# Causal attention: the mask on the transposed scores moves from a TensorE product to a GpSimd select on the exponentials

## The chip, the cores and the metric

The kernel runs on one core of a Trainium2 chip. The metric is the device time of one execution in microseconds (us). The kernel before took 5578.49 us, the median of three runs (5568.84 to 5580.77 us).

## The reference

The program is a chain of twelve layers over an input of 8 sequences x 256 tokens x 128 features in f32. Each layer normalises its input and adds its result to it: mixtures of experts, a recurrent layer, a local attention network of depth 6, and three attentions with 16 heads of 8 features. Only two of the attentions are causal, and only these are touched.

The first one is an ordinary causal softmax attention:

```
scores = einsum('bhqk,bhsk->bhqs', q, k) / sqrt(dk)
causal_mask = triu(ones((s, s), bool), k=1)
scores = where(causal_mask, -1e9, scores)
weights = softmax(scores, -1)
ctx = einsum('bhqs,bhsk->bhqk', weights, v)
```

The last one has rotated queries and keys in the numerator and plain ones in the denominator; the denominator sums over all keys, the mask applies to the quotient only:

```
num = exp(einsum('bhqd,bhkd->bhqk', q_rot, k_rot) * scale)
den = sum(exp(einsum('bhqd,bhkd->bhqk', q, k) * scale), -1, keepdims=True)
attn = where(tril(ones((C, C), bool)), num / den, 0.0)
```

## The kernel before

The 2048 tokens are cut into four groups of two sequences (512 tokens); activations stand with features on the partitions and tokens along the row. The stages run one after the other, and pieces of the neighbouring stage (normalisations, for instance) are drawn from a queue by `pump` (line 438) and put between the products of the present one.

An attention stage (`attention`, line 953) walks over 16 *quads*, that is, four heads of one group, in a software pipeline: step t projects quad t, does the score products of quads before it, and finishes quads still further back. Inside a stage the order on every compute engine is the order of the program: the class `_Ordered` (line 285) chains each instruction of VectorE (DVE), ScalarE (ACT), GpSimd (POOL) and TensorE (PE) to the one issued before it on that engine. So an instruction that waits holds back all later ones of its engine.

In a step there are four *pairs*. A pair handles two heads of one sequence of 256 tokens:

- First attention (`softmax_quads`, line 812; `pair`, line 850). For quad q1 the scores are computed with queries on the partitions (tile `ms`), and DVE takes the largest of each row (`a_mneg`, line 831). In the next step, quad q2, whose maxima are then known and have been folded into its queries (`a_qa`, made in `turn`, line 843), has its scores computed once more with keys on the partitions (tile `ss`), and ACT takes the exponential of them into `a_e` (`soft`, line 756).
- Last attention (`rotated_quads`, line 892; `pair`, line 912). No maxima are needed: `ms` holds the rotated scores, whose exponential goes to `a_e`, and `ss` the plain ones, whose exponential goes to `a_n` and is summed by DVE into the denominator `a_den`.

A tile of `ms`, `ss` or of the projection `pp` takes two banks of PSUM, and three such tiles exist (`mm2=3` in lines 1688 and 1715). Two more banks serve everything else: one accumulator for `av`, and one called `bank`, which holds in turn the transposed tiles, the output projection and the parts of the queue.

With keys on the partitions, the 256 keys of a sequence are two halves of 128. A pair's `ss` (in the last attention its `ms`) holds for each head 384 columns: the first half of the keys against all 256 queries, then the second half against the last 128 queries. The first and the third 128 columns are diagonal blocks, in which the keys behind a query have to go. The function `scores` (line 727) does this on TensorE: ahead of the score products it multiplies a bf16 identity with a bf16 table that holds 0 or -2^100 (`cq` for queries on the partitions, `ck` for keys on the partitions), once per head with 256 columns, as the first term of the sum in PSUM. The score products (f32, 32-row products in four row groups) are added to it, and the exponential turns the rest into zero. The tables are made from f32 constants by `low_masks` (line 700) at the start of each stage, on DVE.

The exponentials are used in `weigh` (line 761), which multiplies them with the values into `av`. It is called twice per quad: for the first sequence right after pair 2 of the same step (line 885 and line 945), and for the second in the next step, after that step's projection (line 875 and line 933). In the first attention the transposes of the maxima (`turn`) stand between. `weighed` copies `av`, `divide` transposes it, divides by the sum of weights and writes `a_ctx`.

GpSimd has in the first attention only the memsets of `value_rows` (line 691) and `max_rows` (line 709) at the start of the stage, and in the last one the memsets and two products for each rotation (lines 1023 and 1026).

Of the kernel before, what the change touches and what calls it, by code (L numbers as in the profile page):

```python
# [24 lines left out]
ALU = mybir.AluOpType  # L25
# [3 lines left out]
P = 128  # L29
# [11 lines left out]
NEG = -float(2.0**100)  # L41
# [11 lines left out]
def _constants():  # L53

    f = np.float32
    p = np.arange(P)
    c = {}
    c["ident"] = np.eye(P, dtype=f)
    c["mean"] = np.full((P, P), 1.0 / P, f)
    c["ones"] = np.ones((P, P), f)  # L60
    c["iota"] = np.tile(np.arange(E, dtype=f), (P, 1))
    c["krow"] = (p % 32 == DH).astype(f)[:, None]
    c["eps"] = np.tile(
        np.array([1e-5, 2e-5, 2.0**-64, 0.5 * SH * math.log(2.0)], f), (P, 1)
    )
    blk = (p[:, None] // 64 == p[None, :] // 64).astype(f)
    c["blkm"] = blk / f(64)

    z = np.zeros((P, 32), f)
    z[:64, :16] = 1.0  # L70
    z[64:, 16:] = 1.0
    c["hsum"] = z
    z = np.zeros((P, 4), f)
    for n, r in enumerate((32, 96, 48, 112)):
        z[r, n] = 1.0
    c["hpick"] = z

    r = np.zeros((P, P), f)
    for m in range(P):
        if m % 2 == 0:  # L80
            r[m + 1, m] = -1.0
        else:
            r[m - 1, m] = 1.0
    c["rot2"] = r

    sel = np.zeros((P, 4, P), f)
    for g in range(4):
        for j in range(4):
            for d in range(DH):
                sel[DH * (4 * g + j) + d, g, 32 * j + d] = 1.0  # L90
    c["sel"] = sel.reshape(P, -1)


    lev = [np.eye(P, dtype=f)]
    for i in range(7):
        n = 2**i
        q = p // n
        lev.append(((q[:, None] % 2 == 0) & (q[None, :] == q[:, None] + 1)).astype(f))
    c["lev"] = np.concatenate(lev, 1)

    c["cq"] = np.where(p[None, :] > p[:, None], f(NEG), f(0))
    c["ck"] = np.where(p[:, None] > p[None, :], f(NEG), f(0))
    one9 = np.zeros((P, 32), f)
    one9[:, DH] = 1.0
    c["one9"] = one9


    i, key = np.arange(32), np.arange(64)
    ok = (key[None, :] >= i[:, None]) & (key[None, :] <= i[:, None] + WIN)
    m = np.zeros((2, 2, 32, 2, 64), f)  # L110
    m[:, 0] = np.where(ok, f(0), f(LNEG))[:, None, :]
    m[:, 1, :, 0, :WIN] = LNEG
    c["lmask"] = m.reshape(P, -1)
    m = np.zeros((2, 2, 32, 4, 32), f)
    m[:, 0] = np.eye(32, dtype=f)[:, None, :]
    m[:, 1, :, 0] = np.eye(32, dtype=f)
    c["lrow"] = m.reshape(P, -1)

    half = np.arange(0, 64, 2, dtype=f)
    inv_freq = f(1.0) / f(10000.0) ** (half / f(64))  # L120
    t = np.arange(S, dtype=f)
    fr = t[:, None] * inv_freq[None, :]
    fr = np.concatenate([fr, fr], -1).T
    base = (half + f(0.4 * 64)) / f(1.4 * 64)
    sc = base[None, :] ** ((t - f(S // 2)) / f(WIN // 2))[:, None]
    sc = np.concatenate([sc, sc], -1).T
    two = lambda a: np.concatenate([_partners(a.T).T] * 2, 0).astype(f)

    sgn = np.where(p[:64, None] < 32, f(-1), f(1))
    c["qcos"] = two(np.cos(fr) * sc * f(8.0))  # L130
    c["qsin"] = two(np.sin(fr) * sc * f(8.0) * sgn)
    c["kcos"] = two(np.cos(fr) * (f(1.0) / sc))
    c["ksin"] = two(np.sin(fr) * (f(1.0) / sc) * sgn)

    i = np.arange(DH // 2, dtype=f)
    th = np.power(f(10000.0), f(-2.0) * (i - f(1.0)) / f(DH))
    ang = t[:, None] * th[None, :]
    per = lambda a: np.tile(np.repeat(a.T, 2, axis=0), (NH, 1)).astype(f)
    c["rcos"] = per(np.cos(ang))
    c["rsin"] = per(np.sin(ang))  # L140

    groups = {
        "c1": ("ident", "mean", "ones", "iota", "krow", "eps"),
        "cs0": ("cq", "ck"),
        "cs1": ("lev", "blkm"),
        "cs2": ("hsum", "hpick", "lmask", "lrow", "qcos", "qsin", "kcos", "ksin"),
        "cs3": ("rot2", "sel", "ck", "one9", "rcos", "rsin"),
    }
    return {n: {k: c[k].astype(f) for k in ks} for n, ks in groups.items()}

# [9 lines left out]
def _partners(w):  # L160

    w = np.asarray(w)
    return w.reshape(w.shape[:-1] + (2, 32)).swapaxes(-1, -2).reshape(w.shape)
# [16 lines left out]
def _layout(inp):  # L180
# [74 lines left out]
    }  # L255
    a, at = {}, {}
    packs = {"pv": pv, "w0": w0, "wt": wt, "w1": w1, "w2": w2, "w3": w3, **_constants()}
    for name, parts in packs.items():
        a[name], at[name] = _pack(parts)
# [49 lines left out]
class _Net:  # L309
# [417 lines left out]
    def scores(self, jobs):  # L727

        parts = {
            None: ((0, 0, 0, S), (1, S, 0, S)),
            "cq": ((0, 0, 0, P), (1, S, 0, S)),
            "ck": ((0, 0, 0, S), (1, S, P, P)),
        }
        for st, a, c, b, heads, mask in jobs:
            if mask is None:
                continue
            for h in range(2):
                blocks = st[:, h, :].rearrange("p (x k) -> p x k", x=4)  # L740
                self.nc.tensor.matmul(
                    blocks[:, 0 :: 3 if mask == "cq" else 2, :], lhsT=self.low["ident"],
                    rhs=self.low[mask].unsqueeze(1).to_broadcast([P, 2, P]),
                    start=True, stop=False, skip_group_check=True)
        for part in range(2):
            for st, a, c, b, heads, mask in jobs:
                half, at, c0, n = parts[mask][part]
                o = b * S
                for h, j in enumerate(heads):
                    r = slice(32 * j, 32 * j + 32)  # L750
                    self.nc.tensor.matmul(
                        st[:, h, at : at + n], lhsT=a[r, o + P * half : o + P * (half + 1)],
                        rhs=c[r, o + c0 : o + c0 + n], start=mask is None, stop=True,
                        skip_group_check=mask is not None)

    def soft(self, st, n):
        e = self.work("a_e", (P, 2, T), bufs=6)
        self.act(e[:, :, :n], st[:, :, :n], AF.Exp, scale=1.0 / math.sqrt(DH))
        return e

    def weigh(self, q, b, causal):
# [532 lines left out]
    def two(self, name):  # L1294
        return self.psp2.tile([P, 2, T], F32, tag="mm2", name=name)
# [383 lines left out]
    def run(self, stages):  # L1679
# [7 lines left out]
        def att0(st):  # L1687
            self.scope(st, "a0", mm=0, acc=1, mm2=3)
            self.value_rows()
            self.max_rows()  # L1690
            self.low_masks(("ident", "cq", "ck"))
            self.attn0()

        def rwkv(st):
# [19 lines left out]
        def att3(st):  # L1714
            self.scope(st, "a3", mm=0, acc=1, mm2=3)
            self.value_rows(ones=False)
            self.low_masks(("ident", "ck"))
            self.attn3()

        makers = (moe0, att0, moe0, None, rwkv, None, local, att2, local, moe3, att3, moe3)  # L1720
        for g in range(NG):
            self.queue.append(self.enter(0, g))
# [56 lines left out]
```

## Time and profile before

| What | Value |
|---|---|
| median of the runs | 5578.49 us |
| the profiled execution | 5561.13 us, span 5559.4 us |
| granted TensorE clock, mean | 0.962 |
| busy share of the span | PE 90%, weight loads 54%, DVE 63%, ACT 44%, POOL 42% |
| first attention | about 275 to 505 us: PE busy 206.5, DVE 110.8, ACT 82.7, POOL 6.2 us |
| last attention | about 5086 to 5374 us: PE busy 241.0, DVE 153.0, ACT 118.1, POOL 25.6 us |
| mask products with `ck` | 128 in each of the two, 0.27 us each as recorded (they overlap) |
| exponentials `a_e` of 768 elements | 64 in each of the two, 0.81 us each |
| maxima `a_mneg` of a pair | 0.42 and 0.68 us as recorded, 1.02 us together |

A line of the groups view names the source line, the engine, the operation, and the tiles as written<-read, with shapes, count, busy time and mean; the line number is mostly that of the helper that records every operation (L300), so the tiles tell the operations apart. A line of the timeline gives start and duration in us; several equal instructions in a row are merged (x2), and the bracket at the end tells how long the engine had been idle before and what released it. The durations of matrix products overlap, so their starts tell more than their lengths. An f32 product is recorded as two.

### The profile page before, as it was taken

To read this page: it belongs to the slowest core of one execution; us is meant where nothing else is said; L and a number is where in the kernel's file an instruction comes from. 1 tells how busy PE (TensorE), PEld (TensorE's weight loads), DVE (VectorE), ACT (ScalarE), POOL (GpSimd) and SP (SyncE) were. 2 spreads that over 40 slices of the span, in tenths; PEclk is the share of its full clock that TensorE was granted. 3 is DMA by queue.
4 is the path that set the end of the run, shared out by engine and by line. 5 is a ranking of instruction groups with operands and counts; after the bars stand their busy time and mean duration, and the time that the engine had idled before them with its cause. 6 is when DMAs were issued, how large, how long until landed. Compare 5 with 4: busy or idle time off the path is not lost.

```text
span 5559.4 us, 161655 instructions
## 1 busy us (share of the span) xinstructions
PE 5031.0 (90%) x73456; PEld 3009.9 (54%) x73456; DVE 3494.9 (63%) x5863; ACT 2440.1 (44%) x2947; POOL 2344.1 (42%) x1205
## 2 busy tenths in 40 slices
PE   9999997899899899988889899989998988899889
PEld 6755754455555555555544455555555555555446
DVE  4444446767767767776645676767767676645555
ACT  2233235444545444444434444545444444433442
POOL 0000022666666666666500666666666666501000
PEclk9999999999999999999989999999999999999999
DMA  1000000111111111111000011111111111000000
GB/s 67 1 1 1 1 1 23 30 35 39 35 40 33 39 34 42 34 35 34 26 23 1 27 38 37 36 40 33 39 34 42 34 35 35 27 34 1 1 1 8
DMA packets 58334, 149.55 MB, mean 27 GB/s; under 512 B 9649, under 2 KB 23858, under 8 KB 57394
## 3 DMA queue, kind: packets, MB, share of 16 engines
q1 hardware_dynamic: 57650, 139.21, 8.3%
q8 instruction: 578, 9.47, 0.7%
q14 instruction: 106, 0.87, 0.1%
HBM read 45.52 MB, written 1.05 MB: 8 GB/s over the span
## 4 chain that ended last, share of the span: by engine, by line
PE 72%; DVE 17%; ACT 6%; issue 4%; POOL 1%; DMA 0%; SPq 0%; DVEq 0%; ACTq 0%; POOLq 0%
PE mm L355 10%; PE pp L300 10%; PE sc L300 7%; PE vp L300 7%; PE e_o L355 6%; PE wo_acc L300 6%; PE bank L300 6%; PE ge L300 5%; DVE l_yr L300 5%; PE cx L300 4%; PE ms L300 3%; PE w_acc L300 2%; DVE l_yk L300 2%; DVE l_yq L300 2%; PE ct L300 2%
## 5 line engine op out<-in xcount | busy, mean ns | idle before, releaser
L300 POOL TENSOR_TENSOR l_yr<-l_yr,l_ksin 128x1024 f32<-128x1024 f32 x192 | 456.8, 2379 | 1024.0 <-DVE l_yr L300 1024.0
L300 PE MATMUL pp<-l_xs,wqkv 128*128 128x512 f32 x1536 | 718.6, 611 | 5.3 <-DMA wqkv<-in_f_wqkv 3.7
L300 ACT COPY l_v<-vp 128x1024 f32<-128x1024 f32 x192 | 194.4, 1013 | 859.3 <-PE vp L300 859.3
L300 ACT ACTIVATE l_sq<-pp 128x1024 f32<-128x1024 f32 x384 | 391.4, 1019 | 283.3 <-PE pp L300 283.3
L300 DVE STREAM_SHUFFLE l_yr<-pp 128x1024 f32<-128x1024 f32 x384 | 505.9, 1318 | 0.0
L300 POOL TENSOR_TENSOR l_e<-l_e,l_rq 128x1024 f32<-128x1024 f32 x192 | 365.7, 1905 | 331.1 <-DVE l_e L300 301.4
L355 PE MATMUL mm<-x,m 128*128 128x512 f32 x1024 | 475.4, 604 | 1.4 <-ACT e_a L387 1.4
L300 DVE TENSOR_REDUCE l_mx<-sc 128x16 f32<-128x1024 f32 x192 | 235.1, 1224 | 374.6 <-PE sc L300 374.6
L300 POOL TENSOR_TENSOR l_yq<-l_yq,l_yr 128x1024 f32<-128x1024 f32 x192 | 456.0, 2375 | 15.0
L300 POOL TENSOR_TENSOR l_yk<-l_yk,l_yr 128x1024 f32<-128x1024 f32 x192 | 453.1, 2360 | 15.1
L300 POOL TENSOR_TENSOR l_yr<-l_yr,l_qsin 128x1024 f32<-128x1024 f32 x192 | 455.1, 2370 | 0.0
L300 PE MATMUL cx<-l_w,l_at 64*32 64x65 f32 x12288 | 304.0, 235 | 148.7 <-ACT l_at L300 123.2
L300 PEld LDWEIGHTS pp<-l_xs,wqkv 128*128 128x128 f32 x1536 | 279.1, 192 | 291.6 <-issue 285.8
L300 PE MATMUL sc<-l_kp,l_yq 64*32 64x64 f32 x24576 | 326.2, 236 | 104.1 <-issue 103.2
L300 PE MATMUL vp<-wqkv,l_xs 128*128 128x256 f32 x1536 | 399.5, 404 | 6.5 <-issue 5.3
L355 PEld LDWEIGHTS e_o<-m,e_h 128*128 128x128 f32 x3072 | 362.9, 192 | 60.6 <-issue 60.1
L300 PEld LDWEIGHTS sc<-l_kp,l_yq 64*32 64x32 f32 x24576 | 277.5, 111 | 172.0 <-issue 170.8
L300 PEld LDWEIGHTS cx<-l_w,l_at 64*32 64x32 f32 x12288 | 261.5, 109 | 197.7 <-ACT l_at L300 137.5
L355 PE MATMUL e_o<-m,e_h 128*128 128x128 f32 x3072 | 363.5, 275 | 0.0
L300 PE MATMUL wo_acc<-l_ct,wo 128*128 128x512 f32 x768 | 358.0, 599 | 0.1
L300 PEld LDWEIGHTS vp<-wqkv,l_xs 128*128 128x128 f32 x1536 | 286.3, 196 | 61.0 <-issue 10.5
L300 PE MATMUL cx<-l_v,l_at 64*32 64x65 f32 x12288 | 309.3, 236 | 6.0 <-issue 6.0
(285 smaller groups left out, 9513.1 us busy)
## 6 DMA issues: line engine op xcount, KB each, us to landing
l_w<-l_v SPq DMA_DIRECT2D x192, 390.0 KB
wqkv<-in_f_wqkv SPq DMA_DIRECT2D x48, 384.0 KB
l_w<-l_v SPq DMA_DIRECT2D x192, 65.0 KB
wo<-in_f_wo SPq DMA_DIRECT2D x12, 512.0 KB
l_rt<-l_rn SPq DMA_DIRECT2D x384, 8.0 KB
m<-in_m_w SPq DMA_DIRECT2D x16, 256.0 KB
w<-in_f_w SPq DMA_DIRECT2D x12, 341.0 KB
w<-in_f_w SPq DMA_DIRECT2D x12, 192.0 KB
```

Of the source, the lines that this page charges most:

```text
L300: r = f(*args, **kw)
L355: self.nc.tensor.matmul(out, lhsT=lhsT, rhs=rhs, start=start, stop=stop)
```

## The change

The `ck` table and its products go. The scores with keys on the partitions are computed without a mask, and the exponential is taken of all 384 columns. After it, GpSimd goes once over the two diagonal blocks of both heads (128 partitions x 512 elements, in place in `a_e`) and writes zero where the key's number, the partition, is greater than the query's, the column. The `weigh` products wait for it. The `cq` products, in front of the scores from which the maxima are taken, remain. The loads of the constants become smaller by one 128x128 table in two groups (cs0 and cs3), and the last attention no longer calls `low_masks`.

```diff
-    c["ck"] = np.where(p[:, None] > p[None, :], f(NEG), f(0))
...
-        "cs0": ("cq", "ck"),
+        "cs0": ("cq",),
...
-        "cs3": ("rot2", "sel", "ck", "one9", "rcos", "rsin"),
+        "cs3": ("rot2", "sel", "one9", "rcos", "rsin"),
...
         for st, a, c, b, heads, mask in jobs:
-            if mask is None:
+            if mask != "cq":
                 continue
             for h in range(2):
                 blocks = st[:, h, :].rearrange("p (x k) -> p x k", x=4)
                 self.nc.tensor.matmul(
-                    blocks[:, 0 :: 3 if mask == "cq" else 2, :], lhsT=self.low["ident"],
+                    blocks[:, 0::3, :], lhsT=self.low["ident"],
                     rhs=self.low[mask].unsqueeze(1).to_broadcast([P, 2, P]),
                     start=True, stop=False, skip_group_check=True)
...
-                        rhs=c[r, o + c0 : o + c0 + n], start=mask is None, stop=True,
-                        skip_group_check=mask is not None)
+                        rhs=c[r, o + c0 : o + c0 + n], start=mask != "cq", stop=True,
+                        skip_group_check=mask == "cq")

     def soft(self, st, n):
         e = self.work("a_e", (P, 2, T), bufs=6)
         self.act(e[:, :, :n], st[:, :, :n], AF.Exp, scale=1.0 / math.sqrt(DH))
+        if n == 384:
+
+            d = e[:, :, :n].rearrange("p j (x k) -> p j x k", x=3)[:, :, 0::2, :]
+            self.nc.gpsimd.affine_select(d, d, pattern=[[0, 2], [0, 2], [1, P]], base=0,
+                                         channel_multiplier=-1, compare_op=ALU.is_ge, fill=0.0)
         return e
...
-            self.low_masks(("ident", "cq", "ck"))
+            self.low_masks(("ident", "cq"))
...
-            self.low_masks(("ident", "ck"))
```

## Prediction

> **What bounds the kernel now.** The change touches two of the twelve stages, so I asked first, with the busy time by stretch, how the engines stand in the steady part of each: the first attention (290 to 490 us) and the last one (5110 to 5370 us).
>
> ```profile
> core 0: us, PE busy (x) PEld busy (x) DVE busy (x) ACT busy (x) POOL busy (x), PEclk, DMA share, GB/s
> 290.00:490.00 200.00, 178.83 (x1845) 108.09 (x1846) 97.50 (x191) 73.03 (x99) 0.00 (x0) 0.94 0.01 1
> 5110.00:5370.00 260.00, 220.02 (x1879) 114.29 (x1877) 142.04 (x164) 114.71 (x138) 13.98 (x11) 0.92 0.00 1
> ```
>
> PE is busy 89% and 85%, GpSimd 0% and 5%. So PE's list of products sets the pace, unless a wait does. Which waits remain is read from the timeline (start, duration, engine, line, operation), here two pairs of the first attention at full clock.
>
> ```profile
> 400.85 0.38 PE L300 MATMUL ms<-low_cq,low_ident 128*128 128x256 bf16 x2
> ...
> 401.40 0.25 DVE L300 RECIPROCAL a_rec<-bank 128x16 f32<-128x16 f32 x1
> 401.55 0.39 PE L300 MATMUL ss<-low_ck,low_ident 128*128 128x256 bf16 x2 [0.31 <-DVE a_mneg L300]
> ...
> 401.87 0.38 PE L300 MATMUL ms<-a_qk 32*128 32x128 f32 x2
> ...
> 402.84 1.02 DVE L300 TENSOR_REDUCE a_mneg<-ms 128x2 f32<-128x256 f32 x2 [0.86 <-PE ss L300]
> 402.90 0.81 ACT L300 ACTIVATE a_e<-ss 128x768 f32<-128x768 f32 x1 [1.22 <-PE ss L300]
> 403.92 0.39 PE L300 MATMUL ss<-low_ck,low_ident 128*128 128x256 bf16 x2 [0.79 <-DVE a_mneg L300]
> ...
> 404.24 0.38 PE L300 MATMUL ms<-a_qk 32*128 32x128 f32 x2
> ...
> 405.11 0.86 PE L300 MATMUL av<-a_e,a_v 128*32 128x256 f32 x16
> ```
>
> Where PE waits, it waits for the maxima (a_mneg) that free the PSUM tile of ss, and the two ck products start right after that wait (0.06 us behind the reduction's end at 403.86). The scores start 0.32 us later. So even where DVE ends last, the ck products stand behind its end, on the path.
>
> **What the removal is worth.** One pair of ck products per pair of heads, 64 in each stage. From the first ck product to the first score product I read each of the 64 pairs from the timeline: median 0.32 us, 0.54 to 0.57 us in the few where the clock was down, sums 21.6 us (first attention) and 22.5 us (last). That is the ceiling: 44 us. It is not all won, since part of the 0.32 us is the change from a whole-array product to 32-row score products, which the products ahead of the masks may now pay. The chain of work, in a pair without a wait, gives the floor:
>
> ```profile
> 410.69 0.32 PE ms L300 x2
> 411.01 0.22 PE ss L300 x2
> ```
>
> The second row is the two ck products following two cq products: 0.22 us. First attention: 22 of the 64 pairs wait for a_mneg (the tile view of ss counts 12.1 us in 22 waits) and win all, 22 x 0.34 = 7.4 us (0.34 is 21.6 / 64); the other 42 win 0.22 to 0.34, I take 0.27: 11.3 us. Together 18.7. Last attention: a mask ahead of a wait wins nothing.
>
> ```profile
> PE bank L300 <- DVE a_ctx L300: 35.6, 14, 2.8
> ```
>
> These 14 waits end on the chain scores, exponential, a_den, a_rec, a_ctx. Where the products in front of the wait are the pair that feeds this chain, the mask counts; where the pair comes between, it is covered, and so are the few pairs whose ss waits for an exponential (at 5133.70 us, for instance). I strike 10 of 64: 54 x 0.30 (middle of 0.22 and 0.35) = 16.2 us. Gross gain 35 us, bounds 26 (floor everywhere, 14 struck) and 44. The removed casts of ck (one per stage) and the 64 KB less in two loads lie beside other work: 0 us; uncovered, the cast would be worth its row, 0.22 us. The cq products of the first attention stay as they are.
>
> **What the select costs.** 128 selects of 128x512 f32 in place on GpSimd, 64 per stage. No such instruction is in the trace. Two views bound it, the groups of GpSimd elsewhere (here 2000 to 2400 us), and its timeline in the last attention:
>
> ```profile
> L300 POOL TENSOR_TENSOR l_e<-l_e,l_rq 128x1024 f32<-128x1024 f32 x22 | 41.9, 1904 | 37.2 <-DVE l_e L300 37.2
> L300 POOL COPY l_xs<-x 64x512 f32<-64x512 f32 x10 | 5.8, 606 | 0.0
> ```
>
> ```profile
> 5094.43 1.26 POOL L300 TENSOR_TENSOR a_rot<-a_y,a_y 128x512 f32<-128x512 f32 x1 [1.68 <-DVE a_y L300]
> ```
>
> A copy of 512 elements per partition (on 64 partitions), one stream in and one out, took 0.61 us: floor. A two-tensor product of 512 took 1.26 us. The select reads one tensor but also forms and compares a counter; nearest is the product with a broadcast operand, 1.90 us for 1024, about 1.0 us for 512. I take X = 1.0 us. The Trainium skill speaks for far more: its GPSIMD Engine Reference, section 3.1, gives some 2.6 cycles an element for two inputs, which the 1.26 us row supports, but about 12 for data-dependent branching. If the select branches per element, 512 x 12 at the 1.2 GHz of its Specifications is an estimate of 5.1 us. No row here is near that, so I keep it only as the upper end.
>
> 64 us of GpSimd in a 230 us stage is no throughput bound. The price is latency: the weighing products (av) now wait for exponential, then select. Queued behind a waiting av on PE is everything: the next pair, its maxima, its exponentials. I took from the timeline the time from the end of the last needed exponential to the start of each of the 32 av groups per stage (above: 402.90 + 0.81 = 403.71 to 405.11, 1.40 us). Those after a pair lose 0.32 us of it with the mask. An av needs X plus about 0.2 us of two handovers (0.15 us from DVE's end at 5094.29 us to the a_rot product on GpSimd, 0.06 us as from a_mneg to PE).
> First attention, slack that remains: 8 groups 1.08 us, 3 at 1.27, 4 over 1.8, 13 behind the transposed maxima 1.37, 2 at 0.46, the last two of the stage none. Last attention: 16 groups after the projection 2.9 (two at its end have none), 3 about 1.1, 2 about 0.8, 2 about 1.4, the others over 1.5.
> With X = 1.0, need 1.2: first attention 8 x 0.12 + 2 x 0.74 + about 2.4 at the end = 4.9 us; last 0.3 + 2 x 0.4 + 2.3 = 3.4 us. Together 8 us. At X = 0.61 about 4 us, at 1.26 about 15, at 1.8 about 35, at 2.0 about 44.
>
> GpSimd's own queue: in the last attention the selects stand in program order between the rotation's products (a_y, a_rot; 12 of them beside the pairs), each 1.27 us, whose inputs come from DVE. A select behind an a_rot that waits for a_y can be late by that 1.27 us, but the av groups of those steps have bank products in front and over 1.5 us of slack: 0 us, at most 12 x 0.5 = 6 us. The memsets at both stage starts end before the first exponential.
>
> A rule speaks against GpSimd beside DVE: the skill's GPSIMD Engine Reference, Specifications, says that it shares its SBUF ports with VectorE, in conflict with two-port modes and two-SBUF-input instructions. This trace shows it: the cast of ck took 1.90 us beside the memset of a_v, and 0.22 us in the other stage without it.
>
> ```profile
> 275.82 1.90 DVE L706 CAST low_ck<-sb_cs 128x128 bf16<-128x128 f32 x1
> ```
>
> By the rule alone all of DVE's stage would be at risk. But in these stages DVE reads PSUM (a_mneg, the copies) or one f32 tensor at its plain rate (a_den, 1.22 us for 1024); x<-ln_c,ln_r with two SBUF inputs comes 4 times per stage. Cost 0 us, at most 8 x 1.0 = 8 us if each waits out a select.
>
> **Sum.** Against the profiled execution (5561.1 us, span 5559.4): 5561 - 35 + 8 = 5534 us. The runs' median, 5578.5 us, is 17 us above this execution; the difference of 27 us is carried over: 5578.5 - 27 = 5552 us.
>
> **The rivals.** (1) Forecast: X below 1.5 us, gain 12 to 38 us, 5541 to 5566. Chance 0.62.
> (2) No change: the saved time turns into the new wait. For X between 1.5 and 2.05 us the stalls (about 25 to 46 us) eat the gross 35; likeliest 5576. For it speaks that most of the first attention's slacks lie within 0.3 us of each other, so that nearly every av starts to wait at once. Against it, the copy's and product's rows. Chance 0.15.
> (3) Slower: the select is long, and each av in the first attention waits. The point is X about 2.05 us, twice my value. At X = 2.4 (a 1024-element product's row, as if the four rows of 128 cost a start each) the need is 2.6 us: stalls 44 us in the first attention and 19 in the last, minus 35: 5606 us. At 5.1 us, stalls 225 us, 5768. Chance 0.23.
> That the mask's products are hidden already is not open for the first attention (they stand behind the wait), and for the last it is in the floor of 26 us.
>
> **How the numbers follow.** A measurement of this kernel can tell about 0.2% (11 us) from no change. Faster by more: case 1, 0.62. Within: 0.15. Slower: 0.23. The range takes case 1, case 2 and the beginning of case 3: 5540 to 5595, leaving out some 0.04 below and 0.15 above. The granted clock, 0.94 and 0.92 in these stretches, can move 500 us by 1%, 5 us; that is within it.
>
> **What would show it.** Right: select rows of 0.6 to 1.3 us on GpSimd; PE's stretch from 290 us on shorter by some 15 us over the first attention and 12 over the last; ss scores starting 0.06 us behind a_mneg's end; waits of av for GpSimd below 12 us in all. Wrong: selects over 2 us, or av waiting for GpSimd in the 13 groups behind the transposed maxima; a larger a_ctx wait in the last attention, with the gain there under 8 us.

## The result and the profile after

The changed kernel took 5551.36 us (median of five runs, 5545.20 to 5556.13), the kernel before beside it 5568.84 us (five runs, 5563.04 to 5580.77). The ratio is 0.9963, 95% interval [0.9946, 0.9979]: 20.6 us faster by the ratio (12 to 30). A second set of runs of the same kernel, below, gave 0.9964 [0.9951, 0.9977]. The forecast was 27 us faster and 5552 us, so the direction was right; the gain came out 6 us smaller, though 27 lies within the interval. That 5552 us was hit almost exactly is luck: the median of before had moved too, from 5578 to 5569 us with two more runs, and from there the forecast gain would have led to 5542 us.

First the row on which the prediction hung. The groups of the kernel after show the select:

```profile
L299 POOL TENSOR_SCALAR_AFFINE_SELECT a_e<-a_e 128x512 f32<-128x512 f32 x128 | 81.5, 637 | 368.2 <-ACT a_e L299 368.2
```

0.64 us each, beside the 0.61 us of the plain copy, at the lower end of my bounds. Next the timeline of two pairs of the first attention at full clock, which answers to the one in the prediction:

```profile
397.25 0.38 PE L299 MATMUL ms<-low_cq,low_ident 128*128 128x256 bf16 x2
397.56 0.49 PE L299 MATMUL ms<-a_qk 32*128 32x128 f32 x4
...
398.80 1.02 DVE L299 TENSOR_REDUCE a_mneg<-ms 128x2 f32<-128x256 f32 x2 [0.43 <-PE ms L299]
...
398.99 0.81 ACT L299 ACTIVATE a_e<-ss 128x768 f32<-128x768 f32 x1 [1.20 <-PE ss L299]
...
399.20 0.49 PE L299 MATMUL ms<-a_qk 32*128 32x128 f32 x4
399.87 0.64 POOL L299 TENSOR_SCALAR_AFFINE_SELECT a_e<-a_e 128x512 f32<-128x512 f32 x1 [1.37 <-ACT a_e L299]
399.97 0.48 PE L299 MATMUL ss<-a_qa,a_qk 32*128 32x256 f32 x2 [0.28 <-DVE a_mneg L299]
...
400.82 0.86 PE L299 MATMUL av<-a_e,a_v 128*32 128x256 f32 x16
```

The scores of ss start right behind the wait for the maxima, with no product between: 0.15 us after the reduction's end at 399.82 us, where before it was 0.06 us to the first ck product and 0.32 us more to the first score. So a pair behind this wait gets its scores 0.23 us earlier, not 0.32. Something else is won: the first ms products of the next quad (399.20 us), which stood behind the ck products, now run ahead of the wait. The exponential ends at 399.80 us, the select at 400.51, the av products start at 400.82: the select is hidden, as it needs 0.71 us of the 1.02 us that are left there. A step without queue work shrank from 11.66 us (av at 405.11 us to 416.77 in the kernel before) to 10.38 us (400.82 to 411.20).

The waits of PE in that stage (us in total, times, longest), one line of before and three of after:

```profile
PE ss L300 <- DVE a_mneg L300: 12.1, 22, 1.5
```

```profile
PE bank L299 <- DVE a_ctx L299: 6.7, 6, 1.2
PE ss L299 <- DVE a_mneg L299: 4.5, 9, 1.4
...
PE av L299 <- POOL a_e L299: 2.2, 3, 1.6
```

Of the 22 waits for the maxima 9 are left in which PE stands idle, and three waits for GpSimd have come, in the last 18 us of the stage (0.35, 0.22 and 1.59 us).

Now the last attention, whole, from the end of the last update of `t` to the table load on ACT that ends the stage. Before, then after (the first number after the stretch is its length; the last but two is the granted clock):

```profile
5085.70:5373.20 287.50, 240.98 (x1946) 122.74 (x1946) 152.46 (x178) 117.25 (x141) 25.64 (x19) 0.91 0.00 1
```

```profile
5082.90:5363.50 280.60, 234.65 (x1812) 118.57 (x1814) 152.35 (x176) 117.60 (x140) 65.88 (x83) 0.86 0.00 1
```

The largest wait of PE there, 35.6 us for `a_ctx` in 14 waits before, is nearly the same after:

```profile
PE bank L299 <- DVE a_ctx L299: 33.1, 14, 2.8
```

With 134 fewer records (128 removed products, the rest records missing in a trace) PE was busy for only 6.3 us less, and the clock went from 0.91 to 0.86. DVE is busy for as long as before (152.5 and 152.4 us): 64 selects beside it show no cost there.

Stage lengths between such landmarks (the first attention from its first memset of `a_v` to its last table load) came out alike in profiles of the same stage, within about 2 us, while the stretch between the two attentions, in which nothing was changed, varies by 21 us from kernel to kernel, from 4582 to 4603 us. So single stages are compared by the profiles, and whole kernels by the ratios.

| kernel | first attention us: length, PE busy, PE waits | clock | last attention us: length, PE busy, PE waits | clock |
|---|---|---|---|---|
| before | 230.2, 206.7, 21.6 | 0.95 | 287.5, 241.0, 46.3 | 0.91 |
| after | 218.0, 198.7, 18.1 | 0.94 | 280.6, 234.7, 45.5 | 0.86 |
| after, again | 218.0, 198.7, 18.3 | 0.94 | 279.6, 232.0, 47.3 | 0.87 |
| no select | 216.4, 198.8, 16.4 | 0.94 | 275.3, 229.1, 45.9 | 0.88 |
| mask and select | 231.8, 207.2, 23.1 | 0.95 | 291.4, 244.1, 47.5 | 0.89 |
| first only | 220.1, 199.0, 20.1 | 0.94 | 288.6, 243.0, 45.5 | 0.89 |
| last only | 230.4, 207.0, 21.8 | 0.95 | 279.6, 232.0, 47.1 | 0.87 |
| two selects | 226.4, 201.6, 23.4 | 0.92 | 276.1, 229.9, 44.8 | 0.89 |
| four selects | 286.5, 221.0, 64.1 | 0.85 | 310.2, 251.5, 58.8 | 0.85 |
| no cq either | 214.2, 187.3, 25.2 | 0.90 | 279.6, 232.0, 47.3 | 0.87 |
| sum later, mask | 229.5, 205.9, 22.0 | 0.96 | 243.3, 226.0, 16.7 | 0.96 |
| sum later, select | 217.9, 198.6, 18.3 | 0.94 | 236.3, 211.4, 24.5 | 0.96 |
| half sum, mask | 229.3, 205.8, 21.6 | 0.96 | 262.7, 233.7, 29.0 | 0.92 |
| half sum, select | 217.9, 198.6, 18.3 | 0.94 | 248.2, 216.2, 30.7 | 0.93 |

(PE waits are the sum of what the waits view lists for PE's products within the stage.) So the gain of the profile pair is 12.2 us in the first attention and 6.9 us in the last. The stretch between was 8.7 us longer than before, which lies within its 21 us.

### The profile page after: what moved, and what is told of

It is laid out like the page before. It is cut to its first block, busy times and chain, and to the rows that moved or that the text cites. A ratio compares the mean times of both kernels' runs of the same rounds, so it can differ in the third digit from the quotient of the medians.

```text
span 5549.6 us, 161374 instructions
## 1 busy us (share of the span) xinstructions
PE 5021.7 (90%) x73200; PEld 3005.0 (54%) x73200; DVE 3495.1 (63%) x5860; ACT 2437.7 (44%) x2947; POOL 2423.6 (44%) x1333
## 4 chain that ended last, share of the span: by engine, by line
PE 72%; DVE 16%; ACT 6%; issue 5%; POOL 1%; DMA 0%; DVEq 0%; ACTq 0%; SPq 0%; POOLq 0%
PE pp L299 10%; PE mm L354 10%; PE vp L299 7%; PE sc L299 7%; PE e_o L354 6%; PE wo_acc L299 6%; PE bank L299 6%; PE ge L299 5%; DVE l_yr L299 4%; PE cx L299 4%; PE ms L299 2%; PE w_acc L299 2%; DVE l_yk L299 2%; DVE l_yq L299 2%; PE ct L299 2%
## 5 line engine op out<-in xcount | busy, mean ns | idle before, releaser
L299 PEld LDWEIGHTS cx<-l_w,l_at 64*32 64x32 f32 x12288 | 260.5, 109 | 198.6 <-ACT l_at L299 138.1
```

Source lines behind the costliest of these rows:

```text
L299: r = f(*args, **kw)
```

## Experiments

My theory at this point (A): the mask products were on the path; the select costs little; in the last attention the clock granted to TensorE fell and took part of the gain back. The rival (B): the products removed there turned into waits, for ACT's exponentials or for a_ctx, or the waits for GpSimd are the price.

**The select left out.** Its line is deleted from the changed kernel; nothing then zeroes the keys behind a query.

> The mask products are gone and the select too, so nothing sets the keys behind a query to zero; this leaves that part of the computation out. Stage lengths are read from the first memset of a_v to the ACT table load that ends the stage (first attention: before 230.2, after 218.0 us) and from the last update of t to the table load (last attention: before 287.5, after 280.4 us). Theory A (the av products really lose what they wait for GpSimd, 12.6 us in the changed kernel): some 8 to 12 us below the changed kernel, first attention about 211, last about 276 us. Rival B (those waits only take the place of others, or the granted clock falls further and takes it back): within 3 us of the changed kernel in the sum of both stages.

5544.06 us, ratio 0.9958 [0.9943, 0.9973]. First attention 216.4, last 275.3 us, that is, 1.6 us and 4.3 to 5.3 us less than with the select. In the first attention this is what PE waits for GpSimd (2.2 us in three waits). In the last it is not: PE's waits are as long as before (45.9 us beside 45.5 and 47.3), and the difference lies in its busy time at another granted clock. So the price of the select as a wait is 3.3 us (2.2 and 1.1), near the 4 us of the slack sum for X = 0.61; the 12.6 us of the expectation are not among PE's waits. Without the select the change would be worth 13.8 us and 12.2 us by stages, 26 us gross where I had put 35 (23 us by the ratio, 15 to 32); 26 was my floor. The ratios of the kernels with and without the select can't be told apart. The 6 to 7 us of the stages lie between theory A's 8 to 12 and rival B's 3.

**The select alone.** The kernel before, with both:

```diff
         self.act(e[:, :, :n], st[:, :, :n], AF.Exp, scale=1.0 / math.sqrt(DH))
+        if n == 384:
+            d = e[:, :, :n].rearrange("p j (x k) -> p j x k", x=3)[:, :, 0::2, :]
+            self.nc.gpsimd.affine_select(d, d, ...)
```

> The kernel before with the select added and the mask products kept: the select's price by itself, where the slack behind pair 2 is still 1.40 us. By the slack sum the need of 0.84 us is met everywhere but at the ends of the two stages: first attention 230 to 232.5 us, last 288 to 290 us, in all 2 to 5 us, which the ratio cannot tell from 1. If a select costs something at every av product (a handover of 0.1 us or more on PE): first attention 233 us or more.

5573.06 us, ratio 1.0016 [1.0004, 1.0027], so 2 to 15 us slower than before, where I had expected no difference that the ratio can tell. Stages 231.8 and 291.4 us, that is, 1.4 to 1.6 and 2.8 to 3.9 us longer than in the kernels with masks alone; the last is 1.4 us above what I expected. The waits for GpSimd, 0.9 and 1.8 us, agree with the slack sum; the rest of the last attention is again busy time, at a clock of 0.89.

**One stage at a time.** Each of these has the change in one of the two attentions and keeps the `ck` products in the other.

> The change in the first attention alone; the last attention keeps its ck products. By the two stage lengths of the changed kernel: 12 us below the kernel before (ratio 0.998), last attention 287 us and unchanged. Rival: if the two stages' gains are not independent (clock carried over from stage to stage), it differs from 12 by more than 4 us in the first stage.

> The change in the last attention alone; the first attention keeps its cq and ck products. By the stage lengths: 7 us below the kernel before (ratio 0.9987), first attention 230 us and unchanged, granted clock in the last attention 0.86 as in the changed kernel. If the low clock of the changed kernel's profile was chance: clock 0.90 or more and a gain of 11 to 13 us in this stage.

First only: ratio 0.9988 [0.9976, 1.0001], not told apart from before, stages 220.1 and 288.6 us. Last only: 0.9981 [0.9967, 0.9995], stages 230.4 and 279.6 us. The stage lengths add up within about 2 us. The clock of the last attention is 0.87 again with the select there, and 0.89 with the mask, where the profile of before had 0.91. So the low clock of the first profile came back, but the fall is 0.02 to 0.05, not 0.05 each time.

**A longer select.** The select line twice, and in the other kernel four times.

> The same select twice in a row on each tile of exponentials, so the select's time is 1.27 us in place of 0.64. The slack sum of the prediction gives 15 us of stalls at 1.27 us against 4 at 0.64: 11 us slower than the changed kernel, 7 of them in the first attention, and most of it at the av groups behind pair 2, whose slack is 1.08 us. Rival: if the slacks move with the select (later maxima, later exponentials), under 4 us.

> Four selects in a row on each tile, 2.5 us in place of 0.64. By the slack sum of the prediction the stalls are some 68 us (48 in the first attention, 20 in the last) against the 20 to 35 us that the mask's removal is worth: 30 to 45 us slower than the kernel before. If slack moves with the stalls, the first attention stays below 250 us and the kernel within 10 us of the one before.

Two selects: 5562.60 us, ratio 0.9989 [0.9980, 0.9999], some 14 us slower than the changed kernel by the ratios. The first attention is 8.4 us longer (7 expected), 5.0 us of it waits for GpSimd; the last is not longer (276.1 us, at a clock of 0.89, with 0.9 us of waits for GpSimd), which the slack sum did not have. Since two selects took less time there than one, a few us of that stage's length can't be put down to the select. Four selects: 5658.66 us, ratio 1.0157 [1.0144, 1.0171], 88 us slower than before, twice what I expected. The waits and the busy times of its first attention say why:

```profile
PE av L299 <- POOL a_e L299: 49.5, 29, 3.9
```

```profile
274.40:560.90 286.50, 221.02 (x1936) 132.23 (x1934) 113.01 (x215) 80.83 (x111) 168.43 (x261) 0.85 0.00 1
```

The waits themselves, 49.5 us, are near what the slack sum gave (48 for 2.5 us; the four take 2.75 us together, for which I estimate some 55 by the same slacks); in the last attention they are 16.0 us (20). What the sum lacked is the clock: it fell from 0.94 to 0.85, and the same 1936 records took 221.0 us in place of 198.7. Here 46 us more of waits made the stage 68.5 us longer.

**The changed kernel again, and without the cq products too.** The second lets the maxima include the keys behind a query on the diagonal blocks, which a softmax allows: the table, its loads and the loop over masked jobs in `scores` are deleted.

> The changed kernel once more, to see how far the stage lengths and the granted clock wander without any change. Theory A (waits, and a lower granted clock that belongs to the denser products): last attention again below 0.90 and about 276 to 281 us, first attention 217 to 220 us, 0.996 to 0.998 of the time before. If the 0.86 of the first profile was chance: 0.91 in the last attention and about 273 us.

> The changed kernel without the cq products too: the maxima of the first attention are then taken over the diagonal blocks with the keys behind a query in them, which a softmax allows. Theory A: the cq products stand ahead of the wait for a_mneg, so that they are covered where PE waits and won where it does not: some 0.6 us a step, 9 us over 16 steps, less some 2 us of new waits for the select (the slack behind pair 2 falls from 1.03 to about 0.75 us): first attention about 211 us, 6 to 8 us below the changed kernel. Rival (every product of PE counts fully): 64 x 0.28, 18 us below.

Again: ratio 0.9964, 218.0 and 279.6 us, clock 0.87. Without cq: 5550.08 us, ratio 0.9961 [0.9947, 0.9976], no difference from the changed kernel that these runs can tell; first attention 214.2 us, 3.8 us shorter (7 expected). PE is busy for 11.4 us less, but the waits for a_mneg rise from 5.0 to 11.4 us (cq stood in front of that wait), and the clock falls from 0.94 to 0.90. Of the 11.4 us, 7.1 come back as waits.

**The sum issued later.** In the last attention a_ctx waited on DVE behind the sum a_den of pair 0, and PE's bank products waited for a_ctx. This moves the sum of pair 0 behind the division, once with the mask and once with the select:

```diff
             if q1:
-                pair(0, q1)
+                add = pair(0, q1)
             if q2:
                 self.divide(q2)
+            if q1:
+                add()
```

> The kernel before with one reordering in the last attention: the sum a_den of pair 0 is issued on DVE after the division of the older quad, so that a_ctx no longer queues behind it and PE's bank products no longer wait for it (35.6 us in 14 waits before). Theory A: these waits fall below 12 us, PE idles less, the granted clock in the last attention rises from 0.91 to 0.95 or more, the stage shrinks from 287.5 to about 268 us. Rival (the bank products wait for the transposes and the next sum instead): above 280 us.

> The same reordering on the changed kernel. Theory A (the idle of the a_ctx waits, which the mask products did not cover but kept short of half clock, took back part of the gain): granted clock in the last attention from 0.86 to 0.95 or more, and the stage is 11 to 14 us shorter than with the mask and the same reordering, in place of the 7 to 8 us between the changed kernel and the one before. Rival (the exponentials on ACT free the PSUM tiles too late, so that a removed product becomes a wait for ACT whatever the clock): the difference of the two stays at 7 us or falls, with over 10 us of waits of ms for a_n.

Mask: 5528.53 us, ratio 0.9922 [0.9907, 0.9937]; the last attention takes 243.3 us in place of 287.5, a far larger gain than expected (268). Select: 5513.00 us, ratio 0.9897 [0.9880, 0.9915], the fastest kernel here: 236.3 us. The last attention in both, mask first:

```profile
5095.20:5338.50 243.30, 226.01 (x1946) 115.79 (x1946) 151.76 (x178) 116.42 (x141) 25.62 (x19) 0.96 0.00 1
```

```profile
5085.30:5321.60 236.30, 211.44 (x1812) 107.51 (x1814) 151.42 (x175) 116.91 (x140) 65.76 (x83) 0.96 0.00 1
```

Taking away 31 us of waits (a_ctx from 35.6 to 4.2; 30 us of all waits) shortened the stage by 44 us, since PE was also busy for less time with the same products, 226.0 us in place of 241.0 at 0.96 in place of 0.91. At one and the same clock, the ck products are worth 226.0 - 211.4 = 14.6 us of PE. That is near the chain's row, 64 x 0.22 = 14.1 us. But the difference of the two stages is 7.0 us, not the 11 to 14 that theory A had: new waits came in, 24.5 us in place of 16.7. With the mask and then with the select:

```profile
PE bank L300 <- DVE a_ctx L300: 4.2, 11, 0.4
...
PE ss L300 <- ACT a_e L300: 1.6, 2, 0.9
```

```profile
PE ss L299 <- ACT a_e L299: 4.8, 6, 1.6
...
PE bank L299 <- DVE a_av L299: 2.8, 10, 0.4
...
PE av L299 <- POOL a_e L299: 1.8, 2, 0.9
```

So in this tighter stage theory A's forecast failed at an equal clock, and rival B holds in that products turn into waits. They are not the waits that it named, of ms for a_n, of which PE has none: of the 7.8 us, 3.2 are for exponentials that still read the PSUM tile of ss, 2.3 for DVE's copy of av, and 1.8 for the select.

**Half of the sum.** The plain exponentials and their sum are taken over the first 256 of a head's 512 columns only; the denominators then sum half of the keys, and those of the second 128 queries are left out.

```diff
-            self.act(e, n, AF.Exp, scale=1.0 / math.sqrt(DH))
+            self.act(e[:, :, :S], n[:, :, :S], AF.Exp, scale=1.0 / math.sqrt(DH))
...
-                e.rearrange("p j (c k) -> p j c k", c=2), AX.X, ALU.add)
+                e[:, :, :S].rearrange("p j (c k) -> p j c k", c=2), AX.X, ALU.add)
```

> The kernel before with half of the last attention's plain exponentials and half of their sum (512 of 1024 elements), so half of the denominator's keys are left out; ACT is lighter by some 0.4 us and DVE by 0.5 us a pair. It is the base for the next run. a_ctx waits about 14 x 0.9 us shorter: stage about 275 us.

> The same halving on the changed kernel; the same half of the denominator is left out. If the wait for ACT's exponentials (ms for a_n 5.5 us, ms and ss for a_e 5 us, pp for a_n 3.3 us in the changed kernel) is what took the last attention's gain, the stage is 13 us or more below the last run's; if it is the clock and the waits for a_ctx, the difference stays at 7 to 9 us unless the clock rises too.

One profile each: 262.7 us with the mask, 248.2 with the select: 14.5 us apart. The clock is nearly equal (0.92 and 0.93), PE's busy time differs by 17.5 us, and the waits hardly (29.0 and 30.7). By the expectation, 13 us or more speaks for the waits for ACT as what took the gain, unless the clock rises too; it did rise, from 0.86 to 0.93 with the select and from 0.91 to 0.92 with the mask. So this pair does not decide between the two. It shows that where neither the clock nor the waits differ, the whole worth of the products arrives.

## Why the prediction was right, point by point

**The products were on the path: right, mis-sized.** Gross gain 26 us by the stages of the kernel without a select, against 35 forecast within 26 to 44. The failing term is the mean worth of a pair of products, which I put at 0.29 us in the first attention (18.7 / 64) and 0.30 in the last. It came out near the chain's row of 0.22 us: 13.8 / 64 in the first attention, 14.6 / 64 = 0.23 in the last at equal clock. The 0.32 us from the first ck product to the first score holds 0.1 us that stays: in the kernel after, with no ck product between, it is still 0.31 us from the first cq product to the first score (397.25 to 397.56 us).

In the first attention this mean hides two kinds of steps. A step without queue work won 1.28 us for its four pairs, 0.32 each, as I had it: 0.22 and 0.39 us in the pairs without a wait, 0.24 and 0.43 behind the maxima. From av group to av group there are three such steps. Most of those with queue work won 0.65 to 1.1 us, and two next to nothing.

**The share struck as covered: nothing of it seen in the last attention, missing in the first.** I struck 10 of 64 pairs in the last attention for waits for a_ctx; in the changed kernel PE's waits there are as long as before (45.5 and 46.3 us in sum), so no removed product shows as a new wait. In the first attention I struck none. There, in the step from 358.83 to 373.19 us before, three pairs won 0.22 us each, and the gain of the one left went into a wait of the queue's product for ACT (ln_sq); such waits are not listed before and sum to 1.1 us in three after.

**The clock: a term named but put at 5 us to either side.** In the last attention PE was busy for 6.3 to 9.0 us less where the removed products are worth some 14. The two kernels with the mask that ran this stage at 0.89 (first only; mask and select) have 243 and 244 us of PE busy, and the one with two selects has 229.9 us at 0.89: 13 to 14 us at equal clock. The changed kernel's waits are as long as before's, so rival B, that the gain turned into waits, does not hold for it; at the lower clock the rest took longer, and 5.6 to 8.3 us of the 14.6 were lost.

The clock records in the traces take two values, 1.0 and 0.5, and in these stages they change only after 3.41 us or a multiple of it. One wait for a_ctx, some 40 us into the stage, cut at these changes, before and then after:

```profile
5125.50:5128.90 3.40, 0.71 (x6) 0.42 (x4) 1.59 (x3) 1.67 (x2) 0.00 (x0) 1.00 0.00 0
5128.90:5132.30 3.40, 3.27 (x12) 1.57 (x16) 0.77 (x2) 0.00 (x0) 0.25 (x1) 0.50 0.00 0
5132.30:5135.70 3.40, 3.40 (x48) 1.92 (x44) 1.11 (x1) 2.86 (x4) 1.02 (x1) 1.00 0.00 0
```

```profile
5122.80:5126.20 3.40, 1.03 (x2) 0.30 (x2) 1.67 (x3) 0.50 (x1) 1.53 (x2) 1.00 0.00 0
5126.20:5129.60 3.40, 3.40 (x29) 2.64 (x30) 0.69 (x1) 1.68 (x2) 1.90 (x2) 0.50 0.00 0
...
5133.00:5136.40 3.40, 3.40 (x19) 1.64 (x12) 0.84 (x2) 1.73 (x2) 0.64 (x1) 0.50 0.02 5
5136.40:5139.80 3.40, 3.40 (x26) 1.31 (x25) 2.55 (x3) 0.00 (x0) 0.00 (x0) 1.00 0.00 0
```

Of the 133 drops to 0.5 in the last attention of the fourteen profiles, 132 follow a stretch of 3.41 us in which PE was idle for 1.47 us or more. A return to 1.0 follows one with at most 0.35 us of idle. The clock did not drop more often in the changed kernel: before has 12 drops and 54.6 us at 0.5, after 10 drops and 78.5 us, as it stayed down longer. With the mask, first only and mask and select have 61.4 and 64.9 us at 0.5; without it, five profiles have 61.4 to 71.7 and four selects 95.6; the two reordered kernels have 17.1 each. So removing the products went with a longer time at half clock, but the two groups touch. Why it stayed down is open: after, 6 of the 13 stretches that another one at 0.5 followed had no idle of PE in them. The Trainium skill (TensorE: Matmul & The Clock Gate, Part 1) has the array at half rate after an idle window of about 3.4 us and at full rate after a busy one, and this case agrees in kind. It warns of gaps beyond that window, and of short ones that come often; here waits of at most 3.1 us went with it.

**The select: right in mechanism, too high in size.** X was 0.64, not 1.0 us, and PE's waits for GpSimd came to 3.3 us for the 4 that the slack sum has at 0.61. With four selects the waits were 49.5 and 16.0 us for 48 and 20. In the last attention with two selects the sum failed: 0.9 us of waits, where it has some 5. The 12 cycles an element of the skill's GPSIMD Engine Reference, an upper end of 5.1 us, have nothing to do with this instruction: it took 0.64 us.

**Ports and queue: right.** DVE's busy time is unchanged beside the selects (152.5 and 152.4 us), and av waits for GpSimd for 1.1 us in two waits in the last attention, where the rotation shares its queue.

**The rivals.** No change and slower were tied to a select of 1.5 to 2.05 us and over. At 1.27 us some 6 us of gain are left (0.9989) of the 20 at 0.64 us; in a straight line, which is an estimate, the crossing lies near 1.5 us, where I had the beginning of no change, and not at 2.05. At 2.5 us the kernel is 88 us slower, not the 30 to 45 of my sum, because PE's clock fell with its waits.

**The signs.** Two of those that I had named came true: select rows of 0.64 us, and waits of av for GpSimd of 3.3 us in all. Three did not: the stages shrank by 12.2 and 6.9 us, not by 15 and 12; the scores of ss start 0.15 us behind the maxima, not 0.06; and a gain below 8 us in the last attention was half of a sign of being wrong, whose other half, a larger wait for a_ctx, did not come (33.1 us for 35.6).

**The net.** 35 - 8 = 27 forecast; 12.2 + 6.9 = 19.1 us by the stages of the first pair of profiles, 20.6 by the ratio. Gain and price were both put too high, so that part of the error cancelled. Two slips in the sum are small: the middle of 0.22 and 0.35 is 0.285, not 0.30 (0.8 us over 54 pairs), and the floor of 26 us belongs to 10 pairs struck; with 14 it is 25.

## What to carry to other kernels

Price a removed product by the chain's row (0.22 us here), not by the distance to the next one of another shape; that was the mean here, while single steps won more or less. Price a moved step by the slack of each consumer, counted consumer by consumer: this sum held within a fifth for the waits at four times the select's length, and missed the clock. And look at the longest idle of TensorE before trimming its work: 31 us of waits removed by reordering one sum were worth 44 us, and where the products were trimmed while the waits stayed, 5.6 to 8.3 of 14.6 us were lost to a longer time at half clock.

## What was not expected of the hardware

The zeroing select runs at the price of a copy (637 ns for 512 elements per partition, the copy 606 to 617). TensorE's granted clock over a stage was lower where work was taken from it (0.91 and 0.89 with the mask, 0.86 to 0.89 without; 0.94 to 0.90 without cq) and rose with waits removed (0.91 to 0.96). In the last attention no wait of PE's products was above 3.2 us; nearly every drop to half clock there followed a stretch of 3.41 us with about 1.5 us of idle or more.
